# A two-layer kernel with a routed feed-forward: the routing of the second group of batches, and the expert slots of the first, are recorded later

## The chip, the cores and the metric

The kernel runs on one core of one Trainium2 chip. The metric is the device time of one execution in microseconds (us), as a median over several runs. Five engines of the core take part, each with a queue of its own that it works through strictly in order: the Tensor engine (PE, matmuls and transposes), the Vector engine (DVE), the Scalar engine (ACT), GpSimd (POOL) and SyncE (SP), which here only issues DMA transfers. An engine waits where the next instruction of its queue needs something that another engine or a transfer has not finished yet, and everything queued behind that instruction waits as well.

## The reference, cut to what matters

The input x is (16, 512, 128) in float32: 16 batches of 512 tokens, 128 features each. Two layers are computed:

```python
xn = layernorm(x)
x  = x + linear_attention(xn) + moe(xn)        # layer 0
xn = layernorm(x)
x  = x + softmax_attention(xn) + channel_mix(xn)   # layer 1
```

The linear attention has 16 heads of width 8, rotary positions and causal running sums; each output row is divided by a normaliser. The part that the change touches most is the mixture of experts, which the reference writes as a sum over all eight experts:

```python
probs = softmax(flat @ router_w.T)             # 8192 tokens, 8 experts
topk_p, topk_i = top_k(probs, 2)
combine = scatter(topk_p / topk_p.sum(-1))     # zero outside the two chosen
for e in range(8):
    out += square(relu(flat @ w_fc[e].T)) @ w_proj[e].T * combine[:, e:e+1]
out += square(relu(flat @ shared_fc.T)) @ shared_proj.T   # the shared expert
```

The hidden width is 512. Layer 1 has softmax attention over causal chunks with a gate computed from the attention's own energy, and a channel mix (a token shift, a sigmoid gate and a squared relu).

## The kernel before

**Tiling.** A batch is four tiles of 128 tokens. The 16 batches are worked on in groups of 3, 4, 4, 3 and 2. The kernel computes only the two chosen experts of each token: the tokens of a group are sorted by expert into slots, tiles of 128 rows that all belong to one expert. Group 0 (batches 0 to 2) has 31 such slots, group 1 (batches 3 to 6) has 39. Slots are worked on in quads of four.

**Four chains of work per group.** Each is a Python generator that records its instructions piece by piece:

- `dispatch(g)` (line 1038) loads each batch (buffer `x_in`, two of them), normalises it (DVE: statistics `ln_st`, `ln_mv`, `ln_rstd`, then `xn`, kept in a pool of four buffers, one batch each), transposes it (PE, then a copy to `xnT`), and multiplies it with the router (`rt_ps`, line 1061; copied to `lg`). Batches 0 and 1 keep `xnT` on the chip; of every later batch it is stored and loaded again as `xnT_in` when its attention begins (line 1504). Then the group's memory of rows is cleared (line 1069), `route` picks the two experts and their shares on DVE, and `places` works out the slot of each token: running counts by two small matmuls `pl_ps`, one more product `pl_both`, and the steps `pl_ef`, `pl_expert`, `pl_slot` on DVE. Finally every tile of tokens is scattered twice, once for each of its experts, into the rows by an indirect DMA that POOL issues (`send`, line 1087). That is 24 scatters for group 0 and 32 for group 1.
- `slot_tiles(g)` (line 1122) loads a quad of slots (`xg`) once all scatters of the group have been done (line 1135), and transposes it (`xgT`). For each slot it loads the weights of its expert (`wf` and `wp`, lines 1146 and 1149; SP reads the expert's number from `pl_expert`; four buffers each) and computes `hg_ps` on PE, relu on ACT, squares `hg` on DVE or POOL, then `yg_ps` on PE, and stores the result.
- `layer0(g)` (line 1541) runs, batch by batch, `first_layer` (line 1499): the linear attention (`qkv`, `qk`, `sc`, masks `am` on DVE, `o`, the division `o0n`, and the turn into heads `ho_a`, `oh_a`) and, one step behind it, `shared_expert` (line 1006): four matmuls `h_ps`, two relus on ACT, two squarings of `h` on DVE in group 0, then 20 matmuls into `y`, and the sum is stored as `x1`. Batches 0 and 1 of group 0 run side by side.
- `layer1(g)` (line 1553) runs layer 1 batch by batch. Its `head` reloads `x1` and adds what the experts gave by indirect gathers on POOL (line 1107).

**What sets the order.** First, lines 1575 to 1595 merge the four chains into one recording order. Each chain has a start and a step in planned microseconds: `begin[g]` and `length[g]` come from fixed costs (38 and 62 for a batch in the two layers, 2.3 for a slot), so `length[0]` is about 185 and `begin[1]` too. The chain whose next piece is due first is recorded next. A chain's groups follow one another, so the piece of group 1 can't be due before group 0's is through.

```python
chains[0].append((early + 0.1 * late, 0.4 * late / steps, dispatch(g)))
start = begin[g] - 0.2 * late if g else 0.25 * length[0]
```

For group 1, `early` is 0 and `late` is `length[0]`: dispatch(1) begins at 18.5 planned us, and the slots of group 0 at 46.

Second, `Program.run` (line 330) plans the recorded instructions with fixed costs on the five engines and writes each engine's queue out. Among the instructions that are ready on an engine the one recorded first goes first (`_rank`, line 407); DVE instructions that empty a PSUM buffer go ahead of others. A buffer of a pool is handed out by the recording order as well. So what is recorded later tends to be queued later, on all engines. SP's queue follows the same planned order. Scatters and gathers are spaced at least 1900 ns apart in the plan (`SPACE`, line 222), and each is tied to the PE instruction that the plan emitted last before it (line 470):

```python
if op.spaced:
    self._behind(i.ins, self.last["PE"], mybir.DependencyClass.Sync)
```

In a trace nearly all instructions carry the line of the helper that emits them (L259), so they are told apart by their tiles' names. The scatters are L1091, the gathers L1110.

Of the kernel before, what the change touches and what calls it, by code (L numbers as in the profile page):

```python
# [486 lines left out]
def two_layers(ctx: ExitStack, tc: tile.TileContext, x, small, const, w_fc, w_proj, out):  # L487
# [25 lines left out]
    def one(name):  # L513
        return ps_one.tile([P, 512], F32, tag="one", name=name)
# [13 lines left out]
    def load_x(b, tag, bufs):  # L528
        xs = p2.tile([P, NT, D], F32, tag=tag, name=f"{tag}_{b}", bufs=bufs)
        SP.dma_start(xs, x[b].rearrange("(t p) d -> p t d", p=P))  # L530
        return xs

    passed = {
        (n, b): memory.tile([P, T], F32, tag=f"{n}{b}", name=f"{n}_{b}")
        for n in ("xnT", "x1") for b in range(B) if n == "x1" or b > 1
    }
# [25 lines left out]
    def w_(name):  # L562
        lo, hi = _STAYS_AT[name]
        return small_sb[:, lo:hi]
# [59 lines left out]
    def strip(vp, t, head):  # L624
        return vp[:, t, head * (PAIR + 2) : head * (PAIR + 2) + 32]
# [19 lines left out]
    def layernorm_T(xs, xT, name, tag, bufs):  # L645

        st = tiny.tile([P, NT, 6], F32, tag="ln_st", name=f"ln_st_{name}")
        mv = tiny.tile([P, NT, 2], F32, tag="ln_mv", name=f"ln_mv_{name}")
        for t in range(NT):
            V.bn_stats(st[:, t, :], xs[:, t, :])  # L650
            V.bn_aggr(mv[:, t, :], st[:, t, :])
        rstd = tiny.tile([P, NT], F32, tag="ln_rstd", name=f"ln_rstd_{name}")
        S.activation(rstd, mv[:, :, 1], AF.Sqrt, bias=eps, scale=1.0)
        V.reciprocal(rstd, rstd)
        xn = p2.tile([P, NT, D], F32, tag=tag, name=f"xn_{name}", bufs=bufs)
        for t in range(NT):
            V.tensor_scalar(
                xn[:, t, :], xs[:, t, :], mv[:, t, 0:1], rstd[:, t : t + 1], ALU.subtract, ALU.mult
            )
        yield  # L660
        pt = one(f"ln_ps_{name}")
        for t in range(NT):
            M.transpose(pt[:, t * P : (t + 1) * P], xn[:, t, :], ident)
        S.copy(xT, pt)
        return xn

    def tiles_of(g):

        return GROUPS[g] * NT, slot_count(GROUPS[g] * NT)

    def route(lg, g):

        gt, _ = tiles_of(g)

        def new(tag, n=E):
            a = tiny.tile([P, GT, n], F32, tag=f"rt_{tag}", name=f"rt_{tag}_{g}", bufs=1)
            return a[:, 0:gt, :]

        def kept(tag):
            a = tiny.tile([P, GT, 1], F32, tag=f"rt_{tag}", name=f"rt_{tag}_{g}", bufs=3)
            return a[:, 0:gt, :]

        def wide(a):
            return a.to_broadcast([P, gt, E])

        mx, sm, m1, m2 = new("mx", 1), new("sm", 1), kept("m1"), kept("m2")
        pr, s1, s2, p_2 = new("pr"), new("s1"), new("s2"), new("p2")

        def row_max(o, i):
            V.tensor_reduce(o.rearrange("p t o -> p (t o)"), i, AX.X, ALU.max)

        def first(o, values, largest):
            V.tensor_tensor(o, values, wide(largest), ALU.is_equal)
            V.tensor_tensor(o, o, wide(rank), ALU.mult)
            row_max(mx, o)
            V.tensor_tensor(o, o, wide(mx), ALU.is_equal)

        row_max(mx, lg)  # L700
        V.tensor_tensor(pr, lg, wide(mx), ALU.subtract)
        S.activation(pr, pr, AF.Exp)
        V.tensor_reduce(sm.rearrange("p t o -> p (t o)"), pr, AX.X, ALU.add)
        V.reciprocal(sm, sm)
        V.tensor_tensor(pr, pr, wide(sm), ALU.mult)
        row_max(m1, pr)
        first(s1, pr, m1)
        V.scalar_tensor_tensor(p_2, s1, -2.0, pr, ALU.mult, ALU.add)
        row_max(m2, p_2)
        first(s2, p_2, m2)  # L710
        V.tensor_tensor(sm, m1, m2, ALU.add)
        V.tensor_scalar_max(sm, sm, 1e-9)
        V.reciprocal(sm, sm)
        V.tensor_tensor(m1, m1, sm, ALU.mult)
        V.tensor_tensor(m2, m2, sm, ALU.mult)
        return s1, s2, m1, m2
# [321 lines left out]
    def dispatch(g):  # L1038

        gt, n_slots = tiles_of(g)  # L1040
        rows = memory.tile([n_slots * P, D], F32, tag=f"rows{g}", name=f"rows_{g}")
        lg = tiny.tile([P, GT, E], F32, tag="lg", name=f"lg_{g}", bufs=1)[:, 0:gt, :]
        xns = []
        for k in range(GROUPS[g]):
            b = FIRST[g] + k
            if b not in x_in:
                x_in[b] = load_x(b, "x_in", 2)

            stays = b < 2
            xnT = p2.tile(  # L1050
                [P, T], F32, tag="xnT_in" if stays else "xnT", name=f"xnT_{b}",
                bufs=2 if stays else 1,
            )
            xns.append((yield from layernorm_T(x_in.pop(b), xnT, f"0_{b}", "xn", max(GROUPS))))
            if stays:
                ready[b] = xnT
            else:
                SP.dma_start(passed["xnT", b], xnT)
            pl = one(f"rt_ps_{b}")
            for t in range(NT):  # L1060
                M.matmul(
                    pl[:, t * E : (t + 1) * E], xnT[:, t * P : (t + 1) * P], w_("router"),
                    start=True, stop=True,
                )
            S.copy(
                lg[:, k * NT : (k + 1) * NT, :].rearrange("p t e -> p (t e)"), pl[:, 0 : NT * E]
            )
            yield
        clear = SP.dma_start(
            rows.rearrange("(n p) d -> p n d", p=P), zeros.to_broadcast([P, n_slots, D])  # L1070
        )

        clear.needs.update(xns[-1].base.writers)
        s1, s2, share1, share2 = route(lg, g)
        yield
        slots, expert = places(s1, s2, g)
        yield
        sent = []
        for k in range(GROUPS[g]):
            for t in range(NT):  # L1080
                for slot in slots:
                    send(rows, slot[:, k * NT + t : k * NT + t + 1], xns[k][:, t, :], clear, sent)
                yield
        rows_in[g] = (rows, sent)
        routed[g] = (slots, (share1, share2), expert)
# [194 lines left out]
    def values(xT, b):  # L1280

        vp = vpads[1 + b % 2]
        pv = one(f"v1_{b}")
        for t in range(NT):
            cols = slice(t * P, (t + 1) * P)
            M.matmul(pv[:, cols], xT[:, cols], w_("wv1"), start=True, stop=True)
        for o in range(2):
            S.copy(
                by_head(vp)[:, :, o::2, o * DH : (o + 1) * DH],
                pv.rearrange("p (t s o d) -> p t s o d", t=NT, o=2, d=DH)[:, :, :, o, :],  # L1290
            )
        return vp
# [217 lines left out]
    def head(b):  # L1510

        if not 0 <= b < B:
            return None
        x1 = p2.tile([P, NT, D], F32, tag="x1", name=f"x1_{b}")
        SP.dma_start(x1.rearrange("p t d -> p (t d)"), passed["x1", b])
        yield from combine(x1, b)
        xp = p2.tile([P, T + 1], F32, tag="xp", name=f"xp_{b}", bufs=2)
        G.memset(xp[:, 0:1], 0.0)
        yield from layernorm_T(x1, xp[:, 1 : T + 1], f"1_{b}", "xn1", 1)
        yield  # L1520
        base = yield from channel_mix(x1, xp, b)
        yield
        vp = values(xp[:, 1 : T + 1], b)
        yield
        qm, ka = yield from operands(xp[:, 1 : T + 1], b, 0)
        return xp, base, vp, qm, ka
# [45 lines left out]
    length = [a + b for a, b in zip(*work)]  # L1572
    begin = [sum(length[:g]) for g in range(groups + 1)]
    chains = [[], [], [], []]
    for g, n in enumerate(GROUPS):
        early, late = (begin[g - 1], length[g - 1]) if g else (-length[0], length[0])
        steps = n * (1 + NT) + 3
        chains[0].append((early + 0.1 * late, 0.4 * late / steps, dispatch(g)))
        start = begin[g] - 0.2 * late if g else 0.25 * length[0]
        steps = 5 * -(-tiles_of(g)[1] // QUAD) + 1  # L1580
        chains[1].append((start, (begin[g] + 0.8 * length[g] - start) / steps, slot_tiles(g)))
        chains[2].append((begin[g], length[g] / (n * LAYER_STEPS[0]), layer0(g)))
        chains[3].append((begin[g + 1], length[g + 1] / (n * LAYER_STEPS[1]), layer1(g)))
    jobs = [[c[0][0], c] for c in chains]
    while jobs:
        job = min(jobs, key=lambda j: j[0])
        _, step, steps = job[1][0]
# [102 lines left out]
```

## Time and profile before

| what | before |
|---|---|
| median of 3 runs | 1696.43 us (1694.8 to 1696.84) |
| the profiled execution | 1693.02 us |
| its span in the profile | 1691.2 us |
| mean granted PE clock | 0.967 |
| PE busy | 1570.6 us (93%) |
| DVE busy | 1221.7 us (72%) |
| ACT busy | 764.7 us (45%) |
| POOL busy | 412.2 us (24%) |
| scatters on POOL (L1091) | 128, mean 1061 ns each |
| gathers on POOL (L1110) | 128, mean 1013 ns each |

The span is the time from the first to the last recorded instruction of one execution; the device time lies a little above it. The slices of the profile cut the span into 40 equal parts of 42.3 us, with a digit for the busy tenths of each engine in each of them; the row PEclk gives the share of full speed that PE's clock was granted. In lists of instructions the columns are start (us), duration (us), engine, line, operation, out and in with their shapes, and in brackets the wait before the instruction with what ended it. In lists of waits they are the total idle time, its count and its longest piece.

### The profile page before, as it was taken

The numbers are of one execution on the slowest core, as the hardware profiler recorded it, in microseconds if no ns is written. First come the engines' busy times: TensorE is split into PE (matmuls) and PEld (weight loads), VectorE is DVE, ScalarE is ACT, GpSimd is POOL, SyncE is SP. The second block draws the span as 40 slices with busy tenths as digits, with TensorE's granted clock in tenths as the row PEclk, the third lists the DMA queues.
The fourth block names the chain that finished last, engine by engine and source line by source line (L and its number), as shares of the span: only waits on it lengthen the run. The fifth ranks groups of instructions, "written<-read, shape, count | busy, mean of one in ns | idle before, by whom it ended". The sixth has DMA issues, their size and how long they took to land.

```text
span 1691.2 us, 36456 instructions
## 1 busy us (share of the span) xinstructions
PE 1570.6 (93%) x14503; PEld 1035.6 (61%) x14503; DVE 1221.7 (72%) x2520; ACT 764.7 (45%) x1175; POOL 412.2 (24%) x389
## 2 busy tenths in 40 slices
PE   4869999999999999999999999999999999999996
PEld 2658876576766566666666656666665566555443
DVE  7845458878478975986668894968587867677673
ACT  2324434544443644444444654453544543534424
POOL 2426053054114321151013321140115010104000
PEclk8879999999999999999999999999999999999888
DMA  5357775343342442332223242313133223010000
GB/s 166 119 165 227 219 223 177 94 128 106 110 117 88 116 144 70 111 109 77 88 78 95 80 129 76 103 55 117 51 90 92 63 72 100 8 45 28 19 1 13
DMA packets 155129, 167.78 MB, mean 99 GB/s; under 512 B 13264, under 2 KB 100688, under 8 KB 154960
## 3 DMA queue, kind: packets, MB, share of 16 engines
q1 hardware_dynamic: 146768, 148.67, 29.6%
q0 software_dynamic: 8192, 16.79, 3.1%
q8 instruction: 114, 1.87, 0.4%
q14 instruction: 55, 0.45, 0.1%
HBM read 123.59 MB, written 41.81 MB: 98 GB/s over the span
## 4 chain that ended last, share of the span: by engine, by line
PE 55%; DVE 12%; ACT 3%; issue 1%; ACTq 0%; DVEq 0%
PE sc L259 11%; PE o L259 10%; PE st L259 8%; PE yg_ps L259 5%; DVE maxima L259 4%; PE hg_ps L259 4%; PE y L259 4%; PE qk L259 3%; PE h_ps L259 2%; ACT ex L259 1%; PE ho_a L259 1%; PE qkv L259 1%; PE oh_a L259 1%; PE cm_r L259 1%; PE mx L259 1%
## 5 line engine op out<-in xcount | busy, mean ns | idle before, releaser
L259 DVE TENSOR_REDUCE maxima<-sc 128x2 f32<-128x768 f32 (+2 forms) x448 | 385.4, 913 | 73.9 <-PE sc L259 70.9
L259 ACT ACTIVATE ex<-st 128x1024 f32<-128x1024 f32 x320 | 312.4, 1025 | 184.8 <-PE st L259 175.5
L259 PE MATMUL sc<-ka,qa 32*128 32x512 f32 (+2 forms) x1792 | 213.8, 516 | 7.2 <-DVE maxima L259 3.5
L259 PE MATMUL st<-qa,ka 32*128 32x384 f32 (+3 forms) x2048 | 208.8, 466 | 9.2 <-ACT ex L259 4.6
L259 DVE TENSOR_TENSOR am<-sc,const_sb 128x1024 f32<-128x1024 f32 x128 | 151.3, 1218 | 86.4 <-PE sc L259 82.7
L259 PEld LDWEIGHTS yg_ps<-wp,hg 128*128 128x128 f32 x1304 | 161.9, 194 | 52.6 <-issue 33.4
L259 PE MATMUL yg_ps<-wp,hg 128*128 128x128 f32 x1304 | 184.1, 285 | 8.2 <-DVE hg L259 1.9
L1091 POOL DMA_INDIRECT rows<-xn,pl_slot x128 | 135.9, 1061 | 205.2 <-PE y L259 38.4
L259 PE MATMUL hg_ps<-xgT,wf 128*128 128x128 f32 x1304 | 176.9, 282 | 7.3 <-DVE maxima L259 2.4
L1110 POOL DMA_INDIRECT back<-results,pl_slot x128 | 129.6, 1013 | 213.9 <-PE st L259 45.5
L259 PEld LDWEIGHTS hg_ps<-xgT,wf 128*128 128x128 f32 x1304 | 160.1, 195 | 30.9 <-issue 13.6
L259 PE MATMUL o<-ex,vpad 128*32 128x512 f32 (+3 forms) x2048 | 174.6, 443 | 1.0 <-ACT oT_a L259 0.6
L259 PEld LDWEIGHTS st<-qa,ka 32*128 32x128 f32 x2048 | 103.3, 185 | 78.7 <-issue 27.9
L259 ACT ACTIVATE hg<-hg_ps 128x1024 f32<-128x1024 f32 x84 | 84.0, 1000 | 123.4 <-PE hg_ps L259 108.7
L259 POOL TENSOR_TENSOR hg<-hg 128x1024 f32<-128x1024 f32 x34 | 65.1, 1916 | 304.5 <-ACT hg L259 304.1
L259 PEld LDWEIGHTS sc<-ka,qa 32*128 32x128 f32 x1792 | 90.2, 187 | 68.8 <-issue 19.2
L259 PEld LDWEIGHTS o<-ex,vpad 128*32 128x32 f32 x2048 | 52.3, 109 | 87.4 <-issue 65.5
L259 ACT COPY oTs<-o 128x256 f32<-128x256 f32 (+1 forms) x96 | 42.7, 444 | 119.8 <-PE o L259 114.6
L259 DVE TENSOR_TENSOR hg<-hg 128x1024 f32<-128x1024 f32 (+1 forms) x50 | 58.3, 1167 | 45.6 <-ACT hg L259 38.6
L259 PE MATMUL sc<-q0m,k0T 32*128 32x256 f32 x1024 | 80.4, 405 | 1.8 <-ACT ex L259 1.3
L259 ACT COPY yg<-yg_ps 128x256 f32<-128x256 f32 x84 | 31.0, 369 | 110.5 <-PE yg_ps L259 87.5
L259 PE MATMUL o<-am,vpad 128*32 128x128 f32 x2048 | 77.9, 279 | 1.9 <-DVE am L259 1.8
(189 smaller groups left out, 2230.1 us busy)
## 6 DMA issues: line engine op xcount, KB each, us to landing
wf<-in_w_fc SPq DMA_DIRECT2D x163, 256.0 KB
wp<-in_w_proj SPq DMA_DIRECT2D x163, 256.0 KB
results<-yg SPq DMA_DIRECT2D x79, 128.0 KB
xg<-rows SPq DMA_DIRECT2D x37, 256.0 KB
rows<-zeros SPq DMA_DIRECT2D x2, 2496.0 KB
x_in<-in_x SPq DMA_DIRECT2D x16, 256.0 KB
x<-x SPq DMA_DIRECT2D x16, 256.0 KB
out<-rr SPq DMA_DIRECT2D x16, 256.0 KB
```

What stands on the lines that cost most here:

```text
L259: return getattr(api, method)(*map(made, args), **{k: made(a) for k, a in kw.items()})
L1091: i = nc.gpsimd.indirect_dma_start(out=rows.made()[:, :], out_offset=bass.IndirectOffsetOnAxis(ap=slot.made(), axis=0), in_=row.made(), in ...
L1110: "POOL", lambda: nc.gpsimd.indirect_dma_start(out=o.made(), out_offset=None, in_=results.made()[:, :], in_offset=bass.IndirectOffsetOnAxi ...
```

## The change

The recorded start of `dispatch` for group 1 goes from 0.1 to 0.3 of `length[0]`, that is from 18.5 to 55.6 planned us; for the other groups it stays at 0.1. The recorded start of `slot_tiles` for group 0 goes from 0.25 to 0.4 of `length[0]`, from 46 to 74 planned us; since the chain is to end at the same planned time, its step becomes smaller. In `head` an assertion is added that the store of `x1` has been recorded before its reload; it adds no instruction. No instruction is added or removed on any engine: only the order within the queues differs, and with it the handing out of buffers and the PE instruction that a scatter is tied to.

```diff
@@ -1512,6 +1512,7 @@
         if not 0 <= b < B:
             return None
         x1 = p2.tile([P, NT, D], F32, tag="x1", name=f"x1_{b}")
+        assert passed["x1", b].base.writers
         SP.dma_start(x1.rearrange("p t d -> p (t d)"), passed["x1", b])
         yield from combine(x1, b)
         xp = p2.tile([P, T + 1], F32, tag="xp", name=f"xp_{b}", bufs=2)
@@ -1575,8 +1576,8 @@
     for g, n in enumerate(GROUPS):
         early, late = (begin[g - 1], length[g - 1]) if g else (-length[0], length[0])
         steps = n * (1 + NT) + 3
-        chains[0].append((early + 0.1 * late, 0.4 * late / steps, dispatch(g)))
-        start = begin[g] - 0.2 * late if g else 0.25 * length[0]
+        chains[0].append((early + (0.3 if g == 1 else 0.1) * late, 0.4 * late / steps, dispatch(g)))
+        start = begin[g] - 0.2 * late if g else 0.4 * length[0]
         steps = 5 * -(-tiles_of(g)[1] // QUAD) + 1
         chains[1].append((start, (begin[g] + 0.8 * length[g] - start) / steps, slot_tiles(g)))
         chains[2].append((begin[g], length[g] / (n * LAYER_STEPS[0]), layer0(g)))
```

## The prediction

> **What bounds the kernel now.** I read the page's head and its forty slices first, then a table of stages, then the Tensor engine's waits and its neighbours' timelines in the stage where the waits are.
>
> ```profile
> span 1691.2 us, 36456 instructions
> PE 1570.6 (93%) x14503; PEld 1035.6 (61%) x14503; DVE 1221.7 (72%) x2520; ACT 764.7 (45%) x1175; POOL 412.2 (24%) x389
> PE   4869999999999999999999999999999999999996
> PEclk8879999999999999999999999999999999999888
> ```
>
> PE sets the time: after the fourth slice it never falls below nine tenths. What it lacks it lacks at the start, where its clock is low as well. By stage (columns: stretch, length, busy time of PE, PEld, DVE, ACT, POOL, then granted clock, DMA share, GB/s):
>
> ```profile
> 26.00:46.00 20.00, 3.08 (x15) 2.63 (x15) 16.88 (x70) 4.60 (x9) 3.52 (x4) 0.53 0.15 50
> 46.00:82.00 36.00, 32.17 (x403) 24.22 (x401) 28.54 (x69) 13.80 (x30) 15.96 (x17) 0.88 0.38 123
> 82.00:131.00 49.00, 33.52 (x230) 28.80 (x231) 24.15 (x82) 11.73 (x18) 13.93 (x13) 0.76 0.53 156
> 131.00:279.00 148.00, 140.70 (x1246) 119.62 (x1244) 88.30 (x157) 57.19 (x104) 57.86 (x52) 0.98 0.70 216
> 279.00:1650.00 1371.00, 1319.12 (x12308) 835.64 (x12310) 1032.64 (x2035) 650.76 (x974) 312.69 (x282) 0.99 0.29 84
> ```
>
> PE is idle 16.9 us in 26 to 46, where DVE routes group 0, and 15.5 us in 82 to 131, where DVE is only half busy. The waits of that second stretch, from the list of waits and DVE's timeline:
>
> ```profile
> PE oh_a L259 <- DVE o0n L259: 6.5, 1, 6.5
> PE o L259 <- DVE o0n L259: 2.4, 1, 2.4
> ```
> ```profile
> 91.52 1.12 DVE L259 TENSOR_SCALAR xn<-x_in,ln_mv,ln_rstd 128x128 f32<-128x128 f32 x4 [6.71 <-DMA rows<-xn,pl_slot]
> 96.01 0.29 DVE L259 TENSOR_REDUCE rt_mx<-lg 128x16 f32<-128x128 f32 x1 [3.38 <-ACT lg L259]
> ...
> 114.88 0.17 DVE L259 CAST pl_expert<-pl_ef 1x39 int32<-1x39 f32 x1
> ...
> 116.47 0.42 DVE L259 TENSOR_TENSOR o0n<-ho_a,den 128x256 f32<-128x256 f32 x1
> ```
>
> DVE waits 6.71 us for the last scatter of group 0, then routes group 1 from 96.0 to 115.1, and only then divides o0n, for which PE's oh_a has waited 6.5 us. PE's other waits here are for the same chain: xn of batch 6 (2.95), its copy (0.7), pl_both (2.64).
>
> **Where the orders differ.** The built orders of the two kernels hold the same instructions. On PE they differ from the two pl_ps matmuls (33.3 us in the trace) to the transpose xgT of group 1's fifth quad (278.6); DVE, ACT, POOL and SP rejoin near there as well, and from then on all are alike. So the change decides how early 278.6 is reached; the stage behind it (1371 us, PE 96%) follows, since no engine's queue there hangs on anything but the shifted others.
>
> **The change, part by part.** The sum is against the profiled 1693.02 us (span 1691.2, 1.8 around it); the median shown, 1696.43, is 3.4 above it, and I carry the difference over to it.
>
> (a) Batch 0's h_ps moves from 124 us to before pl_ps. Four matmuls of 128x512: the two rows at 124.25 and 126.22 start 1.72 us ahead of what follows, so 3.4 us of PE work goes into the 6.86 us hole before pl_ps. The second pair must wait for the ACT copy of the first (1.02 us) and would end near 31.6, before pl_both at 33.1. Gain 3.4; at half clock it would run 0.5 past pl_both.
>
> (b) Its two squarings on DVE (1.23 each) move into 46 to 55, where DVE is nearly full: 2.5 us. Against that half of batch 6's statistics (four pairs of 0.26 and 0.18) and half an xn (0.56) move out of the stretch to 83, while two divisions (0.34 and 0.42 each) move in. Ends 0 and +2.5; I take 1, as DVE has 5 us of small gaps there.
>
> (c) The reason for the gain: group 1's batches 5 and 6 and its route go behind batch 0's finish. After o_1_3 PE now has qkv of batch 2, ho_a, oh_a, y_0 (15 of 20 matmuls) to run while the last scatters land and xg loads; xnT_in of batch 2 is loaded 18th in SP's queue, its buffer free once h_ps has run, near 32 us, ahead of the weights at 43.5. The last scatter is now ordered behind oh_a, about 86 us, and in the old trace the last one issued at 89.16 released DVE at 91.52, so about 89; its xg is not needed before 93.7. Stepping DVE and PE through, hg of the first slots starts near 95 to 97 (before: 97.4) with 11 us more work done: h_ps 3.4, qkv 2.6, ho_a and oh_a 2.0, y_0 4.5, less rt and xgT 1.4.
>
> (d) From there the old PE took 33.9 us to 131.3 for 22 us of work. Idle of the stretch 82 to 131 is 15.5 us, and clock 0.76 means half rate for 0.24 x 2 x 49 = 23.5 us, in which PE ran some 17: 8.5 us lost (yg_ps x16 took 3.62 us at 105.8 and 1.95 at 246.3). Together 24 us. In the new order the route's DVE steps stand between batch 2's masks and slot matmuls have other work ahead of them, so I keep 3 us of the 24: small hand-overs at 80 to 87 and one copy before hg.
>
> (e) New stalls. Batch 2's last masks (am_2_3) and hg_0_1_1's squaring queue behind the eight pl_ef steps (2.2 us by the row at 112.42) on DVE; PE's o_2_3 would come some 1.8 us too early. What does a gap of that size cost in clock? The row:
>
> ```profile
> 250.51 1.16 PE L259 MATMUL hg_ps<-xgT,wf 128*128 128x128 f32 x8 [1.81 <-DMA wf<-in_w_fc]
> ```
> ```profile
> 252.00:260.00 8.00, 7.58 (x30) 5.96 (x31) 7.75 (x26) 4.21 (x7) 3.90 (x4) 0.57 0.59 188
> ```
>
> After 1.81 us (and 0.4 more) the clock fell to half for about 0.43 x 2 x 8 = 6.9 us, 3.4 us lost. The Trainium skill (TensorE: Matmul & The Clock Gate, Part 1) has the clock fall only after an idle window of about 3.4 us, by which this gap would cost 1.8 alone. By the rule the sum is 1.7 better; I take the middle, 3.5, ends 0 and 5.2.
>
> (f) Group 1's 32 scatters move from 112.5 to about 131, each 0.96 us on POOL and each tied to PE's place. Cover: POOL idled 47 us behind them.
>
> ```profile
> 223.86 1.89 POOL L259 TENSOR_TENSOR hg<-hg 128x1024 f32<-128x1024 f32 x1 [47.24 <-ACT hg L259]
> ```
>
> Late next would be xg of group 1, in SP's queue ahead of the loads for slots 30 and on. Between first and last scatter lie about 55 us of PE work (1.8 per scatter; before, 64.1 / 31 = 2.1, waits for PE included), then 6.5 us of slots until xgT against 2.4 landing and 2.5 loading. I take 1 (0 to 4). SP's other movers (xnT_in, x1 stores and reloads, xs) wait for DVE's y sums in front of wf loads that have 4 us of slack: 0, 3 if DVE is late.
>
> Sum: +3.4 - 1 + 24 - 3 - 3.5 - 1 = 19 us gained. Profile 1674, median about 1677.5.
>
> **Rivals.** Half of it: the hand-overs cost more. PE and DVE are both near full in 46 to 95, each gap of 1 to 2 us may open another half-clock window of 3.4 lost; three of them and 2.5 for (b) leave 8: 1688. For it: the clock windows in the trace open after small gaps. Against: after 54 us before, with the same tight pairing, the clock held 1.00 to 82.
>
> No change: the lead is given back at a later common wait, 1696. For it: DMA at 0.70 in 131 to 279, and the same slots in fewer microseconds need some 12% more of it. Against: PE waited for wf only 2.2 us there.
>
> Slower: the scatter train of (f) decides. If each took more than (55 + 6.5 + 19) / 31 = 2.6 us, xg of group 1 and the weights queued behind it on SP would come over 19 us late and PE would starve; at 2.8 us, 1702. Against: the rows between waits show 0.96 us busy and 1.26 from start to start.
>
> **How the numbers follow.** About 0.2% (3.4 us) is what a measurement can tell from no change. Gain of about 19: 0.56 (1669 to 1685). Half: 0.25 (1685 to 1692). None: 0.06. Slower: 0.13. So faster 0.81, same 0.06, slower 0.13; the range to leave out no more than 2 in 10 is 1665 to 1695, the low end from taking (b), (e) and (f) at nothing and (d) whole.
>
> **What would show it.** h_ps of batch 0 near 26 to 32; oh_a without its 6.5 us wait; hg of the first slots near 96; the clock 1.00 from 90 to 130; o_2_3 with a gap of 1 to 2 us near 135; the first group 1 scatter near 131; xgT of group 1's fifth quad near 259 rather than 278.6. The prediction is wrong if that last transpose is not 12 us or more earlier, or if it is and the end isn't.

## The result

The changed kernel takes 1685.84 us (median of five runs, 1683.13 to 1690.52) against 1696.43 us (1693.72 to 1696.84, five runs too): a ratio of 0.9944, with a 95% interval of 0.9926 to 0.9963. So 10.6 us were gained where 19 were forecast. The time lies in the forecast range, but in the span of the rival "half of it", not in the likeliest one.

The page of the changed kernel's profile (this execution took 1683.13 us):

```profile
span 1681.3 us, 36447 instructions
PE 1566.0 (93%) x14503; PEld 1027.3 (61%) x14503; DVE 1220.5 (73%) x2520; ACT 763.4 (45%) x1175; POOL 405.0 (24%) x389
PE   5898889999999999999999999999999999999996
PEclk8899999999999999999999999999999999999888
```

In PE's row the third slice went from 6 to 9, but slices 4 to 6 now read 8 where there were nines. The same by stage (columns as before: stretch, length, busy time of PE, PEld, DVE, ACT, POOL, granted clock, DMA share, GB/s):

```profile
26.00:46.00 20.00, 8.91 (x26) 4.95 (x26) 16.98 (x70) 6.53 (x11) 3.46 (x4) 0.67 0.18 61
46.00:82.00 36.00, 32.92 (x435) 24.01 (x433) 32.21 (x65) 12.76 (x27) 17.64 (x18) 0.87 0.34 111
82.00:131.00 49.00, 47.67 (x481) 40.15 (x481) 36.74 (x99) 21.24 (x41) 3.84 (x4) 1.00 0.69 210
131.00:279.00 148.00, 125.57 (x1035) 105.84 (x1034) 83.79 (x171) 52.34 (x91) 64.50 (x62) 0.99 0.70 214
279.00:1650.00 1371.00, 1319.65 (x12330) 834.27 (x12330) 1026.22 (x2016) 648.72 (x969) 307.37 (x279) 0.98 0.28 83
```

The stretch 82 to 131 is what the prediction said: PE is busy for 47.7 us of 49 (33.5 before), and the clock stands at 1.00 (0.76 before). The surprise is the next row. In 131 to 279 PE is busy for 125.6 us where it was for 140.7: it now idles there.

To follow this I add up, from the trace, PE's work at full speed: its busy time, less half of what was busy while the clock stood at half (work is counted in this way from here on). The two kernels have done, in us,

| up to | before | changed | ahead |
|---|---|---|---|
| 46 us | 17.2 | 19.5 | 2.3 |
| 82 us | 45.6 | 48.5 | 2.9 |
| 131 us | 69.8 | 96.1 | 26.3 |
| 250 us | 183.4 | 192.9 | 9.5 |
| 280 us | 208.3 | 221.0 | 12.7 |

Of 26 us won, 17 were given back between 131 and 250 us. About 3 came again in 250 to 280, where the old profile had a stretch of half clock and the new one has none. From there both kernels have the same order, and the lead stays as it is (the first `st`, a matmul of layer 1's attention, starts at 275.9 instead of 289.0 us: a lead of 13.1 us) until two short stretches of half clock near 929 and 1004 us, which the old profile doesn't have, take 1.7 and 3.0 us of it. The old profile has one near 1604 us that the new one doesn't have, and 1.8 us come back. At the end the profiles are 9.9 us apart.

What PE waits for where the lead is lost, from the list of waits of 131 to 205 us (total, times, longest; the same list of the kernel before has 2.1 us in all):

```profile
PE yg_ps L259 <- DVE hg L259: 6.3, 5, 1.9
PE yg_ps L259 <- issue: 1.8, 1, 1.8
PE yg_ps L259 <- ACT xgT L259: 1.5, 1, 1.5
PE yg_ps L259 <- ACT oTs L259: 1.0, 1, 1.0
PE o L259 <- DVE am L259: 0.7, 1, 0.7
PE hg_ps L259 <- DMA wf<-in_w_fc: 0.7, 1, 0.7
```

The four rows of `yg_ps` are one kind of wait, whatever name stands behind the arrow: 10.6 us in eight pieces, each ending within 0.1 us after a squaring of `hg` on DVE. PE's timeline shows one, first in the changed kernel and then, in the kernel before, what stood at such a place:

```profile
182.44 1.60 PE L259 MATMUL yg_ps<-wp,hg 128*128 128x128 f32 x12 [0.22 <-DVE hg L259]
183.88 1.06 PE L259 MATMUL hg_ps<-xgT,wf 128*128 128x128 f32 x8
184.77 0.61 PE L259 MATMUL yg_ps<-wp,hg 128*128 128x128 f32 x4
187.31 1.22 PE L259 MATMUL yg_ps<-wp,hg 128*128 128x128 f32 x8 [1.93 <-DVE hg L259]
188.32 1.92 PE L259 MATMUL hg_ps<-xgT,wf 128*128 128x128 f32 x8
```

```profile
154.26 1.95 PE L259 MATMUL hg_ps<-xgT,wf 128*128 128x128 f32 x16
156.14 0.41 PE L259 MATMUL o<-am,vpad 128*32 128x128 f32 x4
156.48 0.49 PE L259 MATMUL yg_ps<-wp,hg 128*128 128x128 f32 x2
156.90 1.07 PE L259 MATMUL o<-am,vpad 128*32 128x128 f32 x28
157.90 1.38 PE L259 MATMUL yg_ps<-wp,hg 128*128 128x128 f32 x10
159.21 1.15 PE L259 MATMUL sc<-q0m,k0T 32*128 32x256 f32 x16
160.29 2.05 PE L259 MATMUL yg_ps<-wp,hg 128*128 128x128 f32 x16
```

Between `hg_ps` and `yg_ps` of a pair of slots lie the relu on ACT (184.97 to 185.99 in this example) and the square on DVE (186.03 to 187.25). Before, batch 2's attention (`sc`, `o`) filled these 2.3 us. In the changed kernel most of that attention was spent earlier, and the slots stand alone.

The whole loss adds up so. In 131 to 250 us PE idles 20.5 us (5.4 before). Waits in front of `yg_ps` are 14.2 of them (3.1 before): the eight above, and 3.6 us in three more behind 205 us. Waits for the weights `wf` are 3.6 (none before). The half clock that follows the wait at 187.31, from 188.3 to 191.7, takes another 1.7 us of work. So the hand-overs are some 11 of the 17 us, not all of them.

### The profile page after: what moved, and what is told of

It reads as the page before. It is cut to its first block, busy times and chain, and to the rows that moved or that the text cites. A ratio compares the mean times of both kernels' runs of the same rounds, so it can differ in the third digit from the quotient of the medians.

```text
span 1681.3 us, 36447 instructions
## 1 busy us (share of the span) xinstructions
PE 1566.0 (93%) x14503; PEld 1027.3 (61%) x14503; DVE 1220.5 (73%) x2520; ACT 763.4 (45%) x1175; POOL 405.0 (24%) x389
## 4 chain that ended last, share of the span: by engine, by line
PE 55%; DVE 13%; ACT 3%; issue 1%; ACTq 0%; DVEq 0%
PE sc L259 11%; PE o L259 10%; PE st L259 8%; PE yg_ps L259 5%; DVE maxima L259 4%; PE hg_ps L259 4%; PE y L259 4%; PE qk L259 3%; PE h_ps L259 2%; ACT ex L259 1%; PE ho_a L259 1%; PE qkv L259 1%; PE oh_a L259 1%; PE mx L259 1%; PE cm_r L259 1%
## 5 line engine op out<-in xcount | busy, mean ns | idle before, releaser
L1091 POOL DMA_INDIRECT rows<-xn,pl_slot x128 | 131.4, 1026 | 224.0 <-DVE pl_slot L259 46.8
L1110 POOL DMA_INDIRECT back<-results,pl_slot x128 | 127.2, 994 | 220.2 <-PE st L259 45.6
L259 PE MATMUL sc<-q0m,k0T 32*128 32x256 f32 x1024 | 82.1, 412 | 3.3 <-ACT ex L259 1.4
```

The costliest lines, as they stand in the source:

```text
L259: return getattr(api, method)(*map(made, args), **{k: made(a) for k, a in kw.items()})
L1091: i = nc.gpsimd.indirect_dma_start(out=rows.made()[:, :], out_offset=bass.IndirectOffsetOnAxis(ap=slot.made(), axis=0), in_=row.made(), in ...
L1110: "POOL", lambda: nc.gpsimd.indirect_dma_start(out=o.made(), out_offset=None, in_=results.made()[:, :], in_offset=bass.IndirectOffsetOnAxi ...
```

## The experiments

My theory after the result: the routing's move closes the hole in 82 to 131 us, as forecast, and the hand-over from `hg_ps` through relu and square to `yg_ps` costs most of it back between 131 and 250. Two rivals: that the slots' later start brings the gain or a part of it, and that the pace of the slots is that of their weights' transfers (the DMA share is 0.78 in 131 to 205), the hand-over only seeming to end last. The sets of runs ran beside their own runs of the kernel before, 1689 to 1693 us there, so kernels are compared by their ratio to it. Where nothing else is said, the whole result is computed.

**Each half of the change alone.** The routing of group 1 alone:

```diff
-        start = begin[g] - 0.2 * late if g else 0.4 * length[0]
+        start = begin[g] - 0.2 * late if g else 0.25 * length[0]
```

> Only the routing of group 1 is moved (0.3), the slots of group 0 keep 0.25. Theory A (the gain is the hole in 82 to 131 us, where DVE routed group 1 ahead of o0n, and it takes the routing's move alone to close it; what was lost again behind 131 us comes from group 0's slots being left alone on PE): the hole closes, PE's full-speed work up to 131 us is within 4 us of the changed kernel's 96 us, and as the slots start no later, the median is at or below the changed kernel's: 1680 to 1687. Theory B (both parts are needed, since slots recorded early stand in front of batch 0's finish): half of the gain or less, 1689 to 1697.

The ratio is 0.9930 (0.9909 to 0.9952), 1678.56 us: all of the gain. But not by the way expected. Work up to 131 us is 82.3 us, not within 4 of 96: batch 6's `xn` is still in front of the slots and waits 5.5 us on DVE for the scatters of group 0, PE 3.1 us for it. In exchange less is given back: PE idles 6.5 us in 131 to 250 (20.5 in the changed kernel), and at 250 us the work done is 194.8, against 192.9 there. So a half-closed hole with slots mixed into other work ends up where a closed hole with bare slots does, and the ratio shows nothing that the slots' later start adds.

The slots of group 0 alone:

```diff
-        chains[0].append((early + (0.3 if g == 1 else 0.1) * late, 0.4 * late / steps, dispatch(g)))
+        chains[0].append((early + 0.1 * late, 0.4 * late / steps, dispatch(g)))
```

> Only the slots of group 0 are moved (0.4), the routing of group 1 keeps 0.1. Theory A: the route still stands ahead of o0n on DVE, so oh_a keeps a wait of 4 us or more; the h_ps matmuls of batch 0 still fill the early hole (2 to 3 us), and the median is 1692 to 1699. Theory B (the slots' start carries the gain): 1684 to 1690, and the wait before oh_a is gone.

1692.26 us, ratio 1.0014 (1.0002 to 1.0026): no gain, so the slots' start isn't what helps. Its waits of 82 to 250 us have the row that the routing's move removes:

```profile
PE oh_a L259 <- DVE o0n L259: 8.3, 1, 8.3
```

The early `h_ps` is here too: work up to 46 us is 21.0 (17.2 before), but at 82 it is 41.8 (45.6), since the clock stood at half for 34 us of 37 to 75. (The profiled execution is the slowest of the twelve, 1699.12 us; its times tell less than the median.)

**What the slots wait for.** Two cuts of the changed kernel, each with all queues in the same order. First, the squares of group 0 are shortened to 32 of 1024 columns, so that most of `hg` stays unsquared; the plan is told the whole square's cost:

```diff
-            (V if pair or g == 0 else G).tensor_tensor(o, o, o, ALU.mult)
+            if g == 0:
+                short = o[:, :, 0:16]
...
+                    lambda: nc.vector.tensor_tensor(short.made(), short.made(), short.made(), ALU.mult),
+                    [], [o.base], 150 + 1.04 * len(ws) * FF,
...
+            else:
+                (V if pair else G).tensor_tensor(o, o, o, ALU.mult)
```

> The changed kernel, but group 0's squarings of hg work on 32 columns of each pair of slots, not 1024 (the rest stays unsquared), with the order of every queue kept. Hand-over theory (PE loses 131 to 250 us waiting for relu and square of a pair of slots, as nothing else stands between hg_ps and yg_ps): each of some ten waits of 1 to 1.9 us loses up to 1.1 us, PE idle of 131 to 250 falls from 20.5 to 9 to 13 us, the median falls by 5 to 10 us to 1676 to 1681. Weights theory (PE waits there at the pace of the weights' transfers, and the hand-over only seems to end last): idle stays above 17 us, the median within 3 us of the changed kernel's 1685.8.

1671.51 us, ratio 0.9887 (0.9865 to 0.9909). PE's timeline, the waits of `hg_ps` and `yg_ps` between 145 and 195 us:

```profile
147.17 1.38 PE L259 MATMUL yg_ps<-wp,hg 128*128 128x128 f32 x10 [0.74 <-DVE hg L1181]
151.01 1.38 PE L259 MATMUL yg_ps<-wp,hg 128*128 128x128 f32 x10 [0.89 <-DVE hg L1181]
...
178.16 1.16 PE L259 MATMUL hg_ps<-xgT,wf 128*128 128x128 f32 x8 [1.33 <-DMA wf<-in_w_fc]
182.89 1.16 PE L259 MATMUL yg_ps<-wp,hg 128*128 128x128 f32 x8 [0.89 <-DVE hg L1181]
189.09 2.08 PE L259 MATMUL hg_ps<-xgT,wf 128*128 128x128 f32 x8 [2.35 <-DMA wf<-in_w_fc]
```

The waits of `yg_ps` for `hg` up to 205 us fall from 10.6 to 3.0 us (with one of 0.51 at 195.5), and the lead at the first `st` grows from 13.1 to 15.3. But PE's idle time in 131 to 250 only falls to 16.0 us, less than expected: waits for `wf` grew from 0.7 to 3.7 us. Behind the hand-over a second limit lies close. By the ratios the cut is worth some 9 us, with intervals that don't touch the changed kernel's; the one profile shows only 2.2 of them up to the first `st`, and where the rest comes from is open.

Second, only a quarter of the weights' bytes is loaded, from group 0's fifth slot on, and all four chunks of a slot use it:

```diff
+                if g == 0 and n >= 4:
+                    nc.sync.dma_start(
+                        wf.made()[:, 0:P],
+                        w_fc[:, bass.ds(e, 1), 0:P].rearrange("p o f -> p (o f)"),
+                    )
+                    return nc.sync.dma_start(
+                        wp.made()[:, 0:1, :],
+                        w_proj[:, bass.ds(e, 1), 0:1, :].rearrange("p o f d -> p (o f) d"),
+                    )
```

> The changed kernel, but from group 0's fifth slot on only the first quarter of each expert's two weight matrices is loaded and all four chunks of a slot use it (the result of these slots is that of other weights), with the order of every queue and PE's work kept. Weights theory: PE's idle time in 131 to 250 us falls from 20.5 to under 12 us and the median by 6 to 12 us to 1674 to 1680. Hand-over theory: only the waits for wf go (3.6 us of the 20.5), idle 15 to 18 us, the median falls by 1 to 4 us.

```profile
147.90 1.38 PE L259 MATMUL yg_ps<-wp,hg 128*128 128x128 f32 x10 [1.77 <-DVE hg L259]
...
187.32 1.16 PE L259 MATMUL yg_ps<-wp,hg 128*128 128x128 f32 x8 [1.93 <-DVE hg L259]
195.17 1.60 PE L259 MATMUL yg_ps<-wp,hg 128*128 128x128 f32 x12 [1.48 <-DVE hg L259]
```

The waits for `hg` stand where they stood, with the same lengths to 0.1 us, but for one: at 181 us the wait for `wf` (0.7) is gone, and the next one for `hg` is 0.9 longer. PE idles 20.2 us in 131 to 250, which neither theory's forecast has. As long as the hand-over is there, the weights' bytes don't set the pace. The median doesn't say it as clearly: 1674.93 us, ratio 0.9909 (0.9891 to 0.9927), lower than one would expect with no wait removed, while its profiled execution (1680.02 us) had a smaller lead at the first `st` than the changed kernel (8.9 us, two stretches of half clock at 240 and 271 us). I don't settle that difference; the intervals of the two kernels overlap.

Then both cuts together, to see of what kind the new waits for `wf` are:

> The changed kernel with both cuts: group 0's squares on 32 columns, and from its fifth slot on a quarter of the weights' bytes. With the short squares alone PE waited 3.7 us for wf in 131 to 205 us (0.7 before the cut). If those waits are the time that bytes take, they fall below 1 us here and PE idle of 131 to 250 falls from 16.0 to under 13.5. If they are set by when a buffer comes free and the load can be issued, they stay above 2.5 us and the idle time above 14.5.

A single execution: 1669.64 us. In the waits of 131 to 205 us no row of `wf` is left; its two longest rows are:

```profile
PE yg_ps L259 <- DVE hg L1191: 3.0, 4, 0.9
PE yg_ps L259 <- ACT xgT L259: 1.8, 1, 1.8
```

PE idles 11.2 us in 131 to 250, and the lead at the first `st` is 20.9 us. So once the squares are short, the weights' bytes are the next limit, at some 3 us. Both theories have their place, one behind the other. But both cuts together bring back 7.8 us of lead (20.9 against 13.1), not the whole loss: the relus, and the waits of group 1's first slots, which neither cut touches, stay.

**Why PE's order has `yg_ps` right behind its own `hg_ps`.** The plan might expect the next weights too late. So its rate for transfers is raised in the changed kernel:

```diff
-                    self.moved = max(self.moved, end) + op.later / 250.0
+                    self.moved = max(self.moved, end) + op.later / 400.0
```

> The changed kernel, with the plan's rate for transfers at 400 bytes per ns in place of 250; other orders may change with it all over the kernel. If PE's order puts yg_ps right behind its own hg_ps because the plan expected the next weights late, which on the chip they are not (a quarter of the weights' bytes changed no wait), then the waits of yg_ps for hg in 131 to 250 us fall from 13 to under 6 us and the lead at 280 us rises from 13 to 18 us or more; the median itself may go either way by other stages. If the four weight buffers or the recording order set it, these waits stay above 9 us.

1698.87 us, ratio 1.0065 (1.0045 to 1.0085). The waits for `hg` do go (2.9 us are left in 82 to 250), but this takes their place:

```profile
PE hg_ps L259 <- DMA wf<-in_w_fc: 10.3, 10, 2.1
PE xgT_ps L259 <- DMA xg<-rows: 4.6, 1, 4.6
```

The lead at the first `st` is 6.3 us, not 18. A plan that counts on faster transfers than there are puts `hg_ps` in front, and PE waits for its weights instead. The order that the changed kernel has is not a mistake of the plan's rate. (This edit reorders the later stages as well, so its whole time tells of more than this stage.)

**How far the two starts can be moved.** Slots at 0.3, between the two:

```diff
-        start = begin[g] - 0.2 * late if g else 0.4 * length[0]
+        start = begin[g] - 0.2 * late if g else 0.3 * length[0]
```

> Routing of group 1 at 0.3, slots of group 0 at 0.3 (0.25 in the run with the routing's move alone, 0.4 in the changed kernel). Hand-over theory: slots that start earlier are mixed with batch 2's attention, so PE idles in 131 to 250 us nearer to the 6.5 of the routing alone than to the 20.5 of the changed kernel: 6 to 13; the hole of 82 to 131 lies between the two (1.3 and 6.9); the median is within 4 us of the routing alone by ratio (0.991 to 0.995). Rival (only the hole of 82 to 131 counts): as good as or better than the changed kernel and than the routing alone by 3 us.

1685.06 us, ratio 0.9983 (0.997 to 0.9996): a miss for both. The idle time in 131 to 250 (12.5 us) lies between the two, as the hand-over theory had it, but so little of the hole is closed (82.1 us of work up to 131, like the routing alone) that the middle is worse than either end: the lead at the first `st` is 5.7 us. The start values act through the plan, which picks among the instructions that are ready, and its orders don't blend.

Routing at 0.4, slots at 0.25:

```diff
-        chains[0].append((early + (0.3 if g == 1 else 0.1) * late, 0.4 * late / steps, dispatch(g)))
-        start = begin[g] - 0.2 * late if g else 0.4 * length[0]
+        chains[0].append((early + (0.4 if g == 1 else 0.1) * late, (0.35 if g == 1 else 0.4) * late / steps, dispatch(g)))
+        start = begin[g] - 0.2 * late if g else 0.25 * length[0]
```

> Routing of group 1 at 0.4 (its step a little smaller, so that it ends before group 1's slots begin), slots of group 0 at 0.25. With the routing at 0.3 and the slots at 0.25, batch 6's xn still waits 5.5 us on DVE for the scatters of group 0 and PE 3.1 us for it. If that wait is what is left of the hole, it goes, work up to 131 us rises from 82 to 88 us or more, and the ratio is 0.988 to 0.992. If the slots' early start sets the hole, work up to 131 us stays under 85 and the ratio is 0.992 to 0.996.

1705.23 us, ratio 1.01 (1.0066 to 1.0133): slower, and by the mechanism that the prediction had as its rival of the other sign. The hole isn't closed further (work up to 131 us is 80.0), and the scatters of group 1 run from 173.4 to 227.5 us, the last nine of them at the engine's own pace of 1.26 us. Group 1's first slots wait for the last of them:

```profile
224.96 0.96 POOL L1091 DMA_INDIRECT rows<-xn,pl_slot  x1 [0.30 <-DMA rows<-xn,pl_slot]
226.22 0.95 POOL L1091 DMA_INDIRECT rows<-xn,pl_slot  x1 [0.30 <-issue]
227.48 0.96 POOL L1091 DMA_INDIRECT rows<-xn,pl_slot  x1 [0.30 <-issue]
```

```profile
232.80 1.94 PE L259 MATMUL xgT_ps<-const_sb,xg 128*128 128x128 f32 x8 [15.71 <-DMA xg<-rows]
```

In the changed kernel the last scatter is issued at 189.7 us and PE never waits for `xg` of group 1. With the routing alone it is 198.1. With the slots at 0.25 the cliff lies between 198 and 227 us.

**The changed kernel once more**, beside these:

> The changed kernel itself, beside the others of this set. Ratio to the kernel before as measured first, 0.9944 within 0.002. In its profile the lead over the kernel before is 12 to 14 us from 280 us on. If the two stretches of half clock near 929 and 1004 us of the first profile came by chance, they are not both here again and the lead holds above 11 us to the end; if they belong to the order of the work, both are here and the lead ends near 8 to 10.

1676.69 us, ratio 0.9938 (0.9917 to 0.9958), as before within its interval. Its profile has the lead at 13.6 us at the first `st`, and work up to 131 us is 97.4. The half clock near 997 us is here again, that near 929 isn't. Over the fourteen profiles of this case the first is at its place (shifted by the lead) in eleven and missing in three, the kernel before's among them; the second is there in three or four. So neither belongs to an order alone: most executions have the first, and the profile of the kernel before happened to be without it. Against that same profile the lead is 17.4 us at the end, where the first profile's was 9.9. But the kernel before was faster in this set as well (its median is 1689.36 us, 1696.43 in the first), so at the end two profiles of different sets can be some 7 us apart with nothing changed. Between sets, leads are therefore safest up to the first `st`, and whole times are compared by the ratios.

**A version that keeps more.** Relu and square are issued as two halves, one slot each, so that the first slot's `hg` is ready sooner; the plan sees one step with the old cost, and PE's order stays:

```diff
+            if g == 0 and len(ws) == 2:
+                def relus():
+                    nc.scalar.activation(h[:, 0, :].made(), ph[:, 0, :].made(), AF.Relu)
+                    return nc.scalar.activation(h[:, 1, :].made(), ph[:, 1, :].made(), AF.Relu)
+
+                def squares():
+                    a, b = h[:, 0, :].made(), h[:, 1, :].made()
+                    nc.vector.tensor_tensor(a, a, a, ALU.mult)
+                    return nc.vector.tensor_tensor(b, b, b, ALU.mult)
+
+                program.add("ACT", relus, [ph.base], [o.base], 200 + 0.8 * 2 * FF)
+                program.add("DVE", squares, [], [o.base], 150 + 1.04 * 2 * FF)
+                return h
```

> The changed kernel, computing all of it, but group 0's relu and square of a pair of slots are each issued as two halves, one slot each, with PE's order kept. Hand-over theory: the first slot's square is done 1 to 2 us sooner, the waits of yg_ps for hg in 131 to 205 us fall from 10.6 to 0 to 4 us, waits for wf grow by 1 to 3 us as in the run with short squares, the lead over the kernel before at 280 us rises from 13 to 16 to 20 us, and the ratio is 0.989 to 0.992. If ACT and DVE pay for the 15 more instructions each instead, the lead stays at 12 to 14 us and the ratio at 0.993 to 0.996.

1675.57 us, ratio 0.9913 (0.9884 to 0.9941), and the waits of the list above are cut to pieces like these:

```profile
148.16 0.49 PE L259 MATMUL yg_ps<-wp,hg 128*128 128x128 f32 x2 [0.51 <-DVE hg L1183]
150.96 1.16 PE L259 MATMUL yg_ps<-wp,hg 128*128 128x128 f32 x8 [0.74 <-DVE hg L1182]
...
189.93 1.16 PE L259 MATMUL hg_ps<-xgT,wf 128*128 128x128 f32 x8 [1.47 <-DMA wf<-in_w_fc]
```

3.3 us for `hg` (10.6 before the edit), 2.4 for `wf` (0.7), and a lead of 17.2 us at the first `st`. This confirms the hand-over with the whole computation in place. It is the best of the complete kernels by its median ratio; its interval overlaps with the changed kernel's.

The same halves where only the routing is moved:

> The routing's move alone (slots at 0.25), with the same halves for group 0; all of it is computed. There PE waits only some 3 us for hg in 131 to 205 us, so the halves can bring at most that: ratio 0.990 to 0.994, not under 0.989. A ratio below 0.989 would say that the hand-over costs more than the waits show.

1680.1 us, ratio 0.9946 (0.9927 to 0.9966), a little worse than expected. The waits for `hg` up to 205 us do fall, from 2.7 to 1.0 us, but then PE, sooner at group 1's slots, waits 1.8 us for their `xg` near 205 us, which the routing alone doesn't show. PE's idle time in 131 to 250 is 6.7 us (6.5 without the halves), and nothing is gained.

And halves in all groups, in the changed kernel:

> The changed kernel with relu and square of every pair of slots issued as two halves, in all groups, PE's order kept; all of it is computed. Hand-over theory: from 205 to 250 us, where group 1's slots begin and POOL squares every other pair (1.9 us each), PE's waits of yg_ps for hg fall from 3.6 us to under 2, and the later stages, where PE has other work between, gain next to nothing: the lead at 280 us 17 to 20 us as with group 0's halves alone or up to 2 more, ratio 0.987 to 0.992. If the additional instructions on ACT and DVE cost PE time in the later stages, the lead falls by 2 us or more from 320 to 1400 us and the ratio is 0.992 to 0.997.

1686.57 us, ratio 0.9959 (0.9944 to 0.9974): the second theory of the two. The hand-over at group 1's begin does shrink (0.8 us of waits for `hg` in 205 to 250, 3.6 in the changed kernel), but the lead falls from 16.0 us at the first `st` to 10.8 at 550 us, where PE has other work between anyway. Some 1.6 us of that go with a stretch of half clock at 507 to 511 us that no other profile has. A half costs ACT 0.60 us where the whole costs 1.02, and POOL 1.09 where the whole costs 1.92. That these additional times are the cause was argued from the place of the loss, not shown by itself.

## Why the prediction was right or wrong

The direction, the mechanism of the gain and the range held. The likeliest value did not: 8 us too much gain, because a cost behind the gain was left out.

*(a) and (b), the early `h_ps`.* Right: together +3.4 - 1 forecast, +2.9 us of work at 82 us (1.3 to 3.8 in the other executions that have this order so far). The second pair ends at 34.0 us, at half clock, 2.4 later than I had it.

*(c), the first slots.* Right: `hg` begins at 96.1 us (95 to 97 forecast), with more done before.

*(d), the hole.* Right: 24 - 3 = 21 forecast, 23.4 us of work more in 82 to 131, at a clock of 1.00. I had put it down to the routing's place, though. With the routing alone the stretch holds 14 us more work (43.7 to 82.3 us, against 45.6 to 69.8 before), with the slots alone 7 (41.8 to 72.9): it takes both to close the hole. DVE's timeline shows the order that was read from the built kernel, the divisions first and group 1's routing behind:

```profile
85.12 0.42 DVE L259 TENSOR_TENSOR o0n<-ho_a,den 128x256 f32<-128x256 f32 x1
86.20 0.42 DVE L259 TENSOR_TENSOR o0n<-ho_a,den 128x256 f32<-128x256 f32 x1
...
110.73 0.28 DVE L259 TENSOR_REDUCE rt_mx<-lg 128x16 f32<-128x128 f32 x1
...
129.70 1.37 DVE L259 SCALAR_TENSOR_TENSOR pl_ef<-const_sb,pl_tiles,pl_ef 1x39 f32<-1x39 f32 x5
```

*(e), the new stalls: this is the step that failed.* I followed the new order on PE to `o_2_3`, found one stall there (1.8 us, and with a loss of clock 3.5), and let everything behind it count as shifted. The stall at `o_2_3` came out at 0.7 us, with no loss of clock. But the loss of the stage is 17 us up to 250 (13.6 when the 3.2 us are set off that came again in 250 to 280, where the old kernel's clock was low). I had taken batch 2's attention as work that moves forward, which is a gain of that much where it goes, and never asked what it had covered where it came from. It had covered some ten hand-overs from `hg_ps` to `yg_ps`, eight of them up to 205 us with waits of 0.2 to 1.9 us. Counted as above, such waits are some 11 us of the 17, waits for the weights 3.6 and clock 1.7. The row was there to see: a relu of 1.0 us and a square of 1.2 between two matmuls of a pair. The runs with short squares and with halves show it for group 0: the waits go with the square's length (10.6 to 3.0 us), not with the weights' bytes (11.5 us with a quarter of them).

*(f), the scatters.* Right: the first at 129.8 us (131 forecast), no wait for `xg` of group 1, so the cost is nothing rather than 1. The rival built on it is real, as the routing at 0.4 shows, though not by the price per scatter that I gave as the point where it decides: there the train begins 44 us later.

*The end of the sum.* The fifth quad's transposes, where the orders meet again, lie from 262.9 to 265.4 us instead of from 278.6 to 278.9: the first is 15.7 us earlier, the last 13.6, above the 12 that I had set as the test. But the end is not 12 us earlier: it is 9.9 in the profiles and 10.6 by the medians, so the second half of that test, that the end follows, was not met. In the profiles 4.7 us went behind the first `st` with two stretches of half clock, and 1.8 came back with one of the old profile. Chance has a part in these stretches, as the counts above show, but the second set of runs gives the same 10 us (ratio 0.9938), so it is not shown that chance alone took the 3 us between 13.1 and the end.

*The rivals.* "Half of it" is where the time fell, for a reason of the same family (hand-overs between engines), but in another place: I put them in 46 to 95, where the work up to 82 us shows nothing lost. The place was that of the rival "no change", a lead given back in 131 to 279; the cause that it named, the transfers, is 3.6 us of waits there.

*Clock, rule against row.* I took the middle between the rule of the Trainium skill (TensorE: Matmul & The Clock Gate, Part 1: it falls after an idle window of about 3.4 us) and the row at 250 us, where the clock fell after a wait of 1.81. Neither settles it. In 131 to 187 us of the changed kernel PE had nine waits of 0.2 to 1.8 us, and the clock stayed at 1.00, so blaming one wait of 1.81 was my reading, not something that the row showed. But the next wait, 1.93 us up to 187.31, was followed by half clock from 188.3 to 191.7 (the eight `hg_ps` at 188.32 take 1.92 us, where eight take 1.06 at 183.88), and PE had no idle time of 3.4 us before that fall either. So the traces disagree with the rule where it says how long PE must idle; what decides between 1.8 and 1.9 us they don't show.

## What to carry to other kernels

When work is moved forward into a hole, list what it stood between at its old place: in software pipelines of matmul, relu, square and matmul, work of another batch is the cover of the hand-over, and the engine that sets the time can begin to wait in a stage in which it hardly waited before. A gain in one stage is carried on only as far as the next stage's own pace allows; compare the work done at a common point behind both, not within the stage that gains. Before widening a move that pays, look at the next one in line (here the scatters): the same move one step further cost 1%.

## What the runs showed of the hardware that was not expected

In executions whose first 80 us have the same order, the loss by half clock in 46 to 82 us was 4.0, 5.6, 6.3, 6.1, 6.3, 4.3 and 5.0 us: some 2 us of a kernel's time are decided there by nothing in its order (6.3 and 4.3 were measured on the same chip). And loading a quarter of the bytes of 27 slots' weights changed no wait by more than 0.1 us between 131 and 181 us, though the DMA share of 131 to 205 us fell from 0.78 to 0.42: a share of 0.78 was no bound here, as long as something slower stood in front.
